# A state-space, Fourier and attention network on one core: ScalarE's deferred evictions, its long work and the last hy states

## The chip, the cores and the metric

The kernel runs on one core of one Trainium2 chip. The metric is the device time of one execution in microseconds, from the first instruction of the core to its last. All data is 32-bit floating point, apart from the two feed-forward blocks, which round to 8-bit and 16-bit formats as the reference does.

## The reference, cut to what matters

Four images of 64 x 64 tokens with 96 channels go through four layers.

- Layer 0: group norm, then a selective-scan block: an input projection, a 3 x 3 depthwise convolution with SiLU, scans in four directions, a layer norm, a gate and an output projection, plus the residual.
- Layer 1: a two-dimensional real Fourier transform (64 x 33 tokens, real and imaginary part as channels), the same kind of block, the inverse transform, plus the residual.
- Layers 2 and 3: linear attention and a quantized feed-forward block, with residuals.

The scans take nearly all of the time. In each direction, for each of 192 (layer 0) or 384 (layer 1) channels and each of 16 states:

```python
delta = softplus(dts + bias)
dA = exp(delta * A)
h = h * dA + (delta * u) * B        # a recurrence over the tokens
y = sum over the states of h * C
```

## The kernel before, in words

**Layout.** Channels lie on the 128 partitions in three groups (c = 0, 1, 2): in layer 0 two images share the partitions, in layer 1 one image fills them. Tokens lie along the free dimension. A direction is cut into segments: eight of 512 tokens in layer 0; 512, 512, 384, 384 and 320 in layer 1, in the opposite order for the two backward directions.

**Phases.** `scans` runs six phases: two pairs of images of layer 0, then four images of layer 1. Each has four directions. That makes 144 segments, and a segment has twelve steps: four state groups q of four states, times three channel groups c. There are 1728 steps in all: 1152 at 512 tokens, 384 at 384 and 192 at 320. Projection of the first pair stands ahead of the phases, and the tail of the last image (inverse transform, layers 2 and 3) behind them.

**One step** (the loop at the end of `scans`) has two pairs of states, hx and hy. VectorE runs the four scans (L546) and the product hcy = hy x C (L704). GpSimd computes hcx = hx x C (L686), copies the last hx and hy states of the segment for the next one (`keep_state`, L559), and fills the next step's hy with delta x u x B (`front_b`, L541). ScalarE computes the exponentials (L523) and scales bx (L498), which TensorE transposes into PSUM (L518). TensorE also transposes hcx and hcy and accumulates them over the states (L568). hx and hy have one buffer each. The banks for exponentials and transposes (`room`, tag "ab") are three, in rotation, so the exponential for the next step's first hy state waits for the last hy scan of this one.

**Order.** The engines' orders are fixed by the program (`manual_schedule`): each engine takes its instructions as the loop emits them. Other work is dealt out by generators in three slots of each step: `slot(None)` after the second hx scan, `slot(None)` between the two hy scans, and `slot(LATE)` ahead of hcy. A slot does two things:

- `prepare_more` takes one piece of `prepare`, which readies the next segment. Its pieces are: load u (three slots for the transfer), three matmuls of the x projection (L429), its eviction xs (L433), three products for delta (L439), each with an eviction (L442), the softplus over all three (L444, with a table load before and after), a transpose of xs (L450), its eviction bt (L455), du = delta x u on VectorE (L460), and three groups of transposes of du (L466) with evictions dut (L469). Products and transposes share one PSUM bank, tag "pp". At the start of the segment's last state group, whatever is left is drained at once.
- `E.step` takes one piece of the side task, such as projections and convolutions for later images (L146, L227), norm and gate (L310 to L354), the Fourier transforms (L833 to L896) or the attention and feed-forward blocks (`tokens`, L913 to L1063). It is taken when a counter, raised by a third of the phase's `RATES` entry in each slot, reaches one. Side work shares one PSUM bank, tag "ms". Its evictions are *deferred*: `E.defer` puts them on a list, and the next `E.step` issues them ahead of its own piece.

**Long work.** A softplus or SiLU needs another activation table. Such a piece is announced with `yield BURST` and runs only in `burst()`, which stands behind the step's exponentials and ahead of the second hx scan. In such a step (`long`), the bx work ahead of the hy scans is left out and follows later in the step.

Of the kernel before, what the change touches and what calls it, by code (L numbers as in the profile page):

```python
# [6 lines left out]
F32 = mybir.dt.float32  # L7
# [14 lines left out]
C, P = 3, 128  # L22
SM = 512
LATE, BURST = "late", "burst"

RATES = [0.71, 1.42, 2.55, 1.66, 1.66, 1.66]
EXP_LN = "natural_log_exp_and_others"


class Cfg:  # L30
# [5 lines left out]
    def __init__(self, pre, NI, KI, NR, nat, R, parts, rows, segs, eps):  # L36
        self.pre = pre
        self.NI, self.PI, self.KI = NI, P // NI, KI
        self.DI = C * self.PI
        self.NR, self.L, self.nat = NR, NR * 64, nat  # L40
        self.R, self.M = R, R + 2 * NST
        self.parts = parts
        self.rows = [(sum(rows[:i]), n) for i, n in enumerate(rows)]
        self.segs = [(sum(segs[:i]), n) for i, n in enumerate(segs)]
        self.eps = eps
# [11 lines left out]
class Env:  # L57
# [16 lines left out]
        self.finish()  # L74
        self.task, self.wants = task, None

    def step(self, kind):

        later, self.later = self.later, []
        for fn in later:  # L80
            fn()
        if self.task is None or self.wants not in (None, kind):
            return False
        try:
            self.wants = next(self.task)
        except StopIteration:
            assert not self.later
            self.task = None
        return True
# [277 lines left out]
class Seg:  # L367


    def __init__(self, ph, k, a, S, first, last):  # L370
        self.ph, self.blk, self.cfg = ph, ph.blk, ph.blk.cfg
        self.k, self.a, self.S, self.first, self.last = k, a, S, first, last
        self.rev = k >= 2
        self.nm = f"{self.cfg.pre}_{ph.g}_{k}_{a}"
        self.blocks = [(t, min(P, S - t)) for t in range(0, S, P)]
        full = S // P

        self.runs = [(0, full, P)] + ([(full, full + 1, S % P)] if S % P else [])
        self.bx, self.b, self.c = {}, {}, {}


class Step:
# [7 lines left out]
def scans(tc, ctx, phases, ident):  # L390
# [8 lines left out]
    nc = tc.nc  # L399
    NBK = SM // P  # L400
    NQ = NST // 4
    sp = ctx.enter_context(tc.tile_pool(name="scan", bufs=1))
    ps = ctx.enter_context(tc.tile_pool(name="scanps", bufs=1, space=PSUM))
    E = Env(tc, lambda name: ps.tile([P, 512], F32, name=name, tag="ms"))

    segs = []
    for ph in phases:
        for k in (0, 2, 1, 3):
            order = ph.blk.cfg.segs[::-1] if k >= 2 else ph.blk.cfg.segs
            segs += [Seg(ph, k, a, S, i == 0, i == len(order) - 1) for i, (a, S) in enumerate(order)]  # L410

    def prepare(z):


        blk, cfg, k, S, nm = z.blk, z.cfg, z.k, z.S, z.nm
        rows = cfg.NI * cfg.M

        def room():
            return ps.tile([P, 512], F32, name=f"pp_{nm}", tag="pp")

        z.u = u = sp.tile([P, C, SM], F32, name=f"us_{nm}", tag="us")
        nc.sync.dma_start(out=u[:, :, :S], in_=z.ph.io["u"][k % 2][:, :, z.a : z.a + S])
        z.xd = blk.dram_tile("xd", (rows, SM), nm, bufs=4)
        yield
        yield
        yield
        px = room()
        for c in range(C):
            nc.tensor.matmul(px[:rows, :S], blk.xpw[:, c, k, :], u[:, c, :S], start=(c == 0), stop=(c == C - 1))  # L429
            yield  # L430
        yield
        xs = sp.tile([P, SM], F32, name=f"xs_{nm}", tag="xs", bufs=2)
        nc.scalar.copy(xs[:rows, :S], px[:rows, :S])  # L433
        nc.sync.dma_start(out=z.xd[:, :S], in_=xs[:rows, :S])
        yield
        z.delta = sp.tile([P, C, SM], F32, name=f"delta_{nm}", tag="delta", bufs=2)
        for c in range(C):
            pd = room()
            nc.tensor.matmul(pd[:, :S], blk.dtw[:, k, c * P : (c + 1) * P], xs[:rows, :S], start=True, stop=True)  # L439
            yield  # L440
            yield
            nc.scalar.activation(z.delta[:, c, :S], pd[:, :S], AF.Identity, bias=blk.dtb[:, c, k : k + 1])  # L442
        yield BURST
        nc.scalar.activation(z.delta[:, :, :S], z.delta[:, :, :S], AF.Softplus)  # L444
        nc.scalar.preload_act_table_set(EXP_LN)
        yield
        pb = room()
        pbv = pb[:, : NBK * rows].rearrange("p (b m) -> p b m", b=NBK)
        for i, (t, n) in enumerate(z.blocks):
            nc.tensor.transpose(pbv[:n, i, :], xs[:rows, t : t + n], ident[:rows, :rows])  # L450
        z.bt = sp.tile([P, NBK, rows], F32, name=f"bt_{nm}", tag=f"bt{cfg.pre}", bufs=2)
        yield
        yield
        for lo, hi, n in z.runs:
            nc.scalar.copy(z.bt[:n, lo:hi, :], pbv[:n, lo:hi, :])  # L455
        yield
        yield
        yield LATE
        z.du = sp.tile([P, C, SM], F32, name=f"du_{nm}", tag="du", bufs=2)
        nc.vector.tensor_tensor(z.du[:, :, :S], z.delta[:, :, :S], u[:, :, :S], ALU.mult)  # L460
        yield
        z.dut = sp.tile([P, NBK, C, P], F32, name=f"dut_{nm}", tag="dut", bufs=2)
        for c in range(C):
            pt = room().rearrange("p (b d) -> p b d", b=NBK)
            for i, (t, n) in enumerate(z.blocks):
                nc.tensor.transpose(pt[:n, i, :], z.du[:, c, t : t + n], ident)  # L466
            yield
            for lo, hi, n in z.runs:
                nc.scalar.copy(z.dut[:n, lo:hi, c], pt[:n, lo:hi, :])  # L469
# [82 lines left out]
            ALU.add,  # L552
        )

    def keep_state(st, h, n0):
        z = st.z
        if not z.last:
            e = 0 if z.rev else z.S - 1
            nc.gpsimd.tensor_copy(  # L559
                z.state[st.c][:, n0 : n0 + 2].rearrange("p (j o) -> p j o", o=1), h[:, :, e : e + 1]  # L560
            )

# [43 lines left out]
    with tc.manual_schedule(engines=IN_ORDER):  # L606
# [3 lines left out]
        st = steps[0]  # L610
# [5 lines left out]
        bgen, pgen, pwants, at, due = make_bx(segs[0], 1), none, None, 0, 0.0  # L616

        def prepare_more(kind):

            nonlocal pwants  # L620
            if pwants not in (None, kind):
                return False
            pwants = next(pgen, LATE)
            return True

        def slot(kind):


            nonlocal due
            prepare_more(kind)  # L630
            due = min(due + st.z.ph.rate / 3, 3.0)
            if due >= 1.0:
                due -= E.step(kind)

        def burst():

            if pwants is BURST:
                return prepare_more(BURST)
            if E.wants is BURST:
                E.step(BURST)  # L640
                return True
            return False

        for i, st in enumerate(steps):
            z, q, c, S = st.z, st.q, st.c, st.z.S
            nxt = steps[i + 1] if i + 1 < len(steps) else None
            if q == 0 and c == 0:
                after = segs[at + 1] if at + 1 < len(segs) else None
                if at == 0 or z.ph is not segs[at - 1].ph:
                    if closing:  # L650
                        close_chunk(closing)
                        closing = None
                    z.ph.io["y"] = [z.blk.dram_tile(f"y{j}", (2, z.cfg.L, C * P), z.ph.g) for j in range(2)]
                    E.start(z.ph.side(E))
                open_segment(z, segs[at - 1] if at else None)
                if after and after.ph is not z.ph:
                    E.finish()
                pgen, pwants = prepare(after) if after else none, None
                at += 1
# [8 lines left out]
            hx = sp.tile([P, 2, SM], F32, name=f"hx_{st.nm}", tag="hx")  # L668
# [5 lines left out]
            long = burst()  # L674
# [9 lines left out]
                nxt.px = [transposed(nxt, 0)]  # L684
            hcx = sp.tile([P, 2, SM], F32, name=f"hcx_{st.nm}", tag="hcx", bufs=2)
            nc.gpsimd.tensor_tensor(hcx[:, :, :S], hx[:, :, :S], z.c[q][0][:, :, :S], ALU.mult)  # L686
            keep_state(st, hx, 4 * q)
            first = 0 if long else per - per // 2
            take(bgen, first)
            scan(st, st.hy, 0, st.ay[0], st.hy[:, 0], 4 * q + 2)  # L690
            if nxt:
                nxt.px.append(transposed(nxt, 1))
            slot(None)
            scan(st, st.hy, 1, st.ay[1], st.hy[:, 1], 4 * q + 3)
            keep_state(st, st.hy, 4 * q + 2)
            if nxt:
                front_y(nxt, 0)
            take(bgen, per - first)
# [369 lines left out]
def build(tc, ins, consts, out):  # L1068
    nc = tc.nc
    with ExitStack() as ctx:  # L1070
# [60 lines left out]
        with ExitStack() as inner:  # L1131
# [3 lines left out]
                [  # L1135
                    Phase(blk[0], 0, pairs[0], side((begin0, 1)), RATES[0]),
                    Phase(blk[0], 1, pairs[1], side((end0, 0), (begin1, 0), (begin1, 1)), RATES[1]),
                    Phase(blk[1], 0, single[0], side((end0, 1), (begin1, 2), (begin1, 3)), RATES[2]),
                    Phase(blk[1], 1, single[1], side((end1, 0)), RATES[3]),
                    Phase(blk[1], 2, single[2], side((end1, 1)), RATES[4]),  # L1140
                    Phase(blk[1], 3, single[3], side((end1, 2)), RATES[5]),
                ],
# [116 lines left out]
```

## Time and profile before

The median of three runs is 12,892.95 us (12,887.82 to 12,930.84).

| engine | busy, us | share of the span |
|---|---|---|
| TensorE | 9942.2 | 77% |
| VectorE | 10,425.9 | 81% |
| ScalarE | 9022.7 | 70% |
| GpSimd | 9126.6 | 71% |

| part of the span | us |
|---|---|
| ahead of the phases | 546 |
| phases 0 and 1 (layer 0) | 2559, 2639 |
| phases 2 to 5 (layer 1) | 1818, 1600, 1604, 1595 |
| behind the phases | 548 |

| group of instructions | count | busy, us | mean, ns |
|---|---|---|---|
| GpSimd hy product, L541 | 1728 | 3707.9 | 2146 |
| GpSimd hcx product, L686, its largest row | 1637 | 3558.6 | 2174 |
| GpSimd copy of hy states, L559 | 1392 | 1365.4 | 981 |
| GpSimd copy of hx states, L559 | 1392 | 322.2 | 231 |
| ScalarE table loads, L444 and L445 | 288 | 369.6 | 1283 |

PE is TensorE, DVE is VectorE, ACT is ScalarE, POOL is GpSimd, SP issues the transfers. A row of the profile's timeline gives start and duration in us, engine, line, operation, what is written and read, and in brackets the engine's idle time before it and what ended that. A row of the list of waits gives who waited for whom: us in total, number of times, the longest. L numbers are lines of the kernel before.

### The profile page before, as it was taken

The page shows a single profiled execution, that of the slowest core. Times are in us where ns is not written, and L with a number is a line of the kernel's source. Part 1 is how long each engine was busy: PE and PEld are TensorE (multiplying, and loading weights), DVE is VectorE, ACT ScalarE, POOL GpSimd, SP SyncE. Part 2 cuts the span into 40 slices and gives each one's busy share as a digit, 9 for nine tenths or more (in the row PEclk, how much of TensorE's full clock was granted, in tenths as well). Part 3 has the DMA queues.
Part 4 walks back from the last instruction along what each step waited for, and adds up shares of the span by engine and source line. Part 5 has one row for each costly group of instructions (what it writes and reads, how often), then busy time and mean ns, then how long its engine had stood idle before and what let it go on. Part 6 is the DMA issues. An engine that isn't in the chain of part 4 may idle for free.

```text
span 12908.9 us, 162342 instructions
## 1 busy us (share of the span) xinstructions
PE 9942.2 (77%) x54680; PEld 7205.1 (56%) x54680; DVE 10425.9 (81%) x10170; ACT 9022.7 (70%) x17333; POOL 9126.6 (71%) x6620
## 2 busy tenths in 40 slices
PE   4677777777777888878888878877788777887766
PEld 1355555555656666556655556555565555655544
DVE  1399999899999888898675688788987989879833
ACT  1478888888787888886565677677776777667723
POOL 0398989898888888886575687666876667766620
PEclk8788898888998999988798888777887778887775
DMA  4344444444555545544443344322433224432231
GB/s 119 104 128 121 123 119 124 116 117 130 144 138 129 135 126 129 140 133 140 124 129 102 120 135 116 101 79 80 135 114 97 80 83 134 113 100 78 81 96 26
DMA packets 1264685, 1464.23 MB, mean 113 GB/s; under 512 B 494243, under 2 KB 1027055, under 8 KB 1255143
## 3 DMA queue, kind: packets, MB, share of 16 engines
q1 hardware_dynamic: 1263847, 1453.85, 40.4%
q8 instruction: 430, 7.05, 0.2%
q14 instruction: 408, 3.34, 0.1%
HBM read 1217.05 MB, written 236.50 MB: 113 GB/s over the span
## 4 chain that ended last, share of the span: by engine, by line
PE 24%; DVE 23%; ACT 21%; POOL 20%; issue 7%; DMA 5%; SPq 0%; POOLq 0%; DVEq 0%; ACTq 0%
POOL hy_l L541 13%; DVE hy_l L546 12%; DVE hx_l L546 5%; PE pc_l L227 4%; ACT ax_l L523 4%; PE acc_l L568 4%; ACT bx_l L498 4%; POOL state_l L559 4%; DVE hcy_l L704 4%; POOL hcx_l L686 2%; ACT b_l L523 2%; PE b_l L518 2%; ACT ab_l L523 2%; PE pp_l L439 2%; PE pi_l L146 1%
## 5 line engine op out<-in xcount | busy, mean ns | idle before, releaser
L541 POOL TENSOR_TENSOR hy_l<-du_l,bc_l 128x1024 f32<-128x1024 f32 (+2 forms) x1728 | 3707.9, 2146 | 1526.5 <-DVE hcy_l L704 1056.2
L686 POOL TENSOR_TENSOR hcx_l<-hx_l,bc_l 128x1024 f32<-128x1024 f32 (+2 forms) x1637 | 3558.6, 2174 | 609.6 <-DVE hx_l L546 607.8
L498 ACT ACTIVATE bx_l<-dut_l,bt_l 128x192 f32<-128x192 f32 (+2 forms) x6272 | 2768.5, 497 | 0.0
L568 PE MATMUL acc_l<-ident,hcy_l 128*128 128x128 f32 (+1 forms) x12120 | 1888.6, 305 | 487.2 <-DVE hcy_l L704 483.9
L546 DVE TENSOR_TENSOR_SCAN hx_l<-ax_l,state_l,b_l 128x512 f32<-128x512 f32 (+2 forms) x1697 | 1839.1, 1125 | 390.2 <-PE b_l L518 315.9
L523 ACT ACTIVATE ax_l<-delta_l,l_alog 128x512 f32<-128x512 f32 (+2 forms) x3456 | 2138.6, 666 | 0.0
L523 ACT ACTIVATE b_l<-delta_l,l_alog 128x512 f32<-128x512 f32 (+2 forms) x1961 | 1229.9, 627 | 1282.9 <-DVE hx_l L546 886.0
L546 DVE TENSOR_TENSOR_SCAN hy_l<-b_l,state_l,hy_l 128x512 f32<-128x512 f32 (+2 forms) x1697 | 1858.3, 1130 | 257.5 <-POOL hy_l L541 126.9
L568 PEld LDWEIGHTS acc_l<-ident,hcy_l 128*128 128x128 f32 (+1 forms) x12120 | 1585.5, 157 | 854.5 <-DVE hcy_l L704 649.1
L568 PE MATMUL acc_l<-ident,hcx_l 128*128 128x128 f32 (+1 forms) x12126 | 1950.4, 311 | 123.8 <-POOL hcx_l L686 121.2
L568 PEld LDWEIGHTS acc_l<-ident,hcx_l 128*128 128x128 f32 (+1 forms) x12126 | 1619.7, 160 | 526.5 <-POOL hcx_l L686 253.1
L704 DVE TENSOR_TENSOR hcy_l<-hy_l,bc_l 128x1024 f32<-128x1024 f32 (+2 forms) x1636 | 1857.5, 1135 | 43.7
L559 POOL COPY state_l<-hy_l 128x2 f32<-128x2 f32 x1392 | 1365.4, 981 | 574.8 <-DVE hy_l L546 553.3
L518 PE MATMUL b_l<-ident,bx_l 128*128 128x128 f32 x6872 | 1240.2, 309 | 526.1 <-DVE hy_l L546 311.9
L523 ACT ACTIVATE ab_l<-delta_l,l_alog 128x512 f32<-128x512 f32 x1314 | 906.3, 690 | 998.6 <-DVE hx_l L546 707.3
L518 PEld LDWEIGHTS b_l<-ident,bx_l 128*128 128x128 f32 x6872 | 867.2, 155 | 1008.6 <-DVE hy_l L546 447.9
L546 DVE TENSOR_TENSOR_SCAN hy_l<-ab_l,state_l,hy_l 128x512 f32<-128x512 f32 x978 | 1205.8, 1269 | 130.7 <-POOL hy_l L541 75.1
L546 DVE TENSOR_TENSOR_SCAN hx_l<-ax_l,state_l,ab_l 128x512 f32<-128x512 f32 x979 | 1197.0, 1264 | 135.1 <-PE ab_l L518 102.1
L518 PE MATMUL ab_l<-ident,bx_l 128*128 128x128 f32 x5260 | 901.8, 307 | 520.9 <-DVE hy_l L546 266.5
L518 PEld LDWEIGHTS ab_l<-ident,bx_l 128*128 128x128 f32 x5260 | 653.1, 155 | 837.7 <-DVE hy_l L546 387.1
L227 PE MATMUL pc_l<-pad_l,l_dg 128*128 128x512 f32 (+2 forms) x1944 | 846.4, 578 | 58.2 <-ACT uh_l L216 42.8
L439 PE MATMUL pp_l<-xs_l,l_dtw 76*128 76x512 f32 (+3 forms) x864 | 525.2, 693 | 194.4 <-ACT delta_l L442 181.9
(190 smaller groups left out, 12231.5 us busy)
## 6 DMA issues: line engine op xcount, KB each, us to landing
bc_l<-l_xd_l SPq DMA_DIRECT2D x1536, 256.0 KB
bc_l<-l_xd_l SPq DMA_DIRECT2D x384, 512.0 KB
bc_l<-l_xd_l SPq DMA_DIRECT2D x384, 384.0 KB
us_l<-l_u SPq DMA_DIRECT2D x96, 768.0 KB
l_y<-y_l SPq DMA_DIRECT2D x288, 256.0 KB
bc_l<-l_xd_l SPq DMA_DIRECT2D x192, 320.0 KB
yt_l<-l_y SPq DMA_DIRECT2D x264, 192.0 KB
yt_l<-l_y SPq DMA_DIRECT2D x128, 384.0 KB
```

What stands on the lines that cost most here:

```text
L146: self.nc.tensor.matmul(out[i * cfg.PI : (i + 1) * cfg.PI, :n], wi[:, ki, half, :], xin[:, max(i, ki), :n], start=(ki == 0), stop=(ki == c ...
L227: nc.tensor.matmul(pc[:, : n * 64].rearrange("p (r w) -> p r w", w=64), diag[:, t, :], pad[:, r - p0 + dy : r - p0 + dy + n, dx : dx + 64] ...
L439: nc.tensor.matmul(pd[:, :S], blk.dtw[:, k, c * P : (c + 1) * P], xs[:rows, :S], start=True, stop=True)
L498: nc.scalar.activation(t[:n, b, :, ch], z.dut[:n, b, :, ch], AF.Copy, scale=z.bt[:n, b, m : m + 1])
L518: nc.tensor.transpose(pb[:, t : t + n], st.z.bx[st.q, j][:n, b, st.c], ident[:n, :n])
L523: nc.scalar.activation(out, z.delta[:, st.c, : z.S], AF.Exp, scale=z.blk.A[:, st.c, z.k, n : n + 1])
L541: nc.gpsimd.tensor_tensor(st.hy[:, :, :S], du, st.z.b[st.q][:, :, :S], ALU.mult)
L546: nc.vector.tensor_tensor_scan(h[:, j, : z.S][:, ::step], a[:, : z.S][:, ::step], b[:, : z.S][:, ::step], 0.0 if z.first else z.state[st.c ...
L559: nc.gpsimd.tensor_copy(z.state[st.c][:, n0 : n0 + 2].rearrange("p (j o) -> p j o", o=1), h[:, :, e : e + 1])
L568: nc.tensor.matmul(z.acc[st.c][:n, b, :], hc[:, j, t : t + n], ident, start=(n0 + j == 0 and b == 0), stop=(n0 + j == NST - 1 and b == 0), ...
L686: nc.gpsimd.tensor_tensor(hcx[:, :, :S], hx[:, :, :S], z.c[q][0][:, :, :S], ALU.mult)
L704: nc.vector.tensor_tensor(hcy[:, :, :S], st.hy[:, :, :S], z.c[q][1][:, :, :S], ALU.mult)
```

## The change

Five edits go together.

1. `flush` is split from `E.step`, and `burst()` calls it ahead of long work, so that deferred evictions stand in front of the softplus or SiLU on ScalarE and not behind it.
2. In a step with long work the middle slot only flushes; it takes no new piece and does not raise the counter. `RATES` is raised by about 3% to make up for it.
3. In `prepare` the delta products are taken apart: a slot lies between the eviction of one and the next product, which needs the same bank.
4. u of the next segment is loaded in the same phase as soon as du has been computed, the last reader of the one u buffer; its three slots of waiting then fall away.
5. The last hy states are copied by ScalarE; in a step with long work GpSimd still does it.

```diff
-RATES = [0.71, 1.42, 2.55, 1.66, 1.66, 1.66]
+RATES = [0.73, 1.47, 2.63, 1.72, 1.72, 1.72]
...
+    def flush(self):
         later, self.later = self.later, []
         for fn in later:
             fn()
+
+    def step(self, kind):
+        self.flush()
         if self.task is None or self.wants not in (None, kind):
             return False
...
+    def load_u(z):
+        z.u = sp.tile([P, C, SM], F32, name=f"us_{z.nm}", tag="us")
+        nc.sync.dma_start(out=z.u[:, :, : z.S], in_=z.ph.io["u"][z.k % 2][:, :, z.a : z.a + z.S])
...
-        z.u = u = sp.tile([P, C, SM], F32, name=f"us_{nm}", tag="us")
-        nc.sync.dma_start(out=u[:, :, :S], in_=z.ph.io["u"][k % 2][:, :, z.a : z.a + S])
         z.xd = blk.dram_tile("xd", (rows, SM), nm, bufs=4)
-        yield
-        yield
-        yield
+        if z.u is None:
+            load_u(z)
+            yield
+            yield
+            yield
+        u = z.u
...
             nc.scalar.activation(z.delta[:, c, :S], pd[:, :S], AF.Identity, bias=blk.dtb[:, c, k : k + 1])
+            if c < C - 1:
+                yield
         yield BURST
...
         nc.vector.tensor_tensor(z.du[:, :, :S], z.delta[:, :, :S], u[:, :, :S], ALU.mult)
+        if z.after and z.after.ph is z.ph:
+            load_u(z.after)
         yield
...
-        def slot(kind):
+        def slot(kind, hold=False):
             nonlocal due
+            if hold:
+                E.flush()
+                return
             prepare_more(kind)
...
         def burst():
+            if BURST in (pwants, E.wants):
+                E.flush()
             if pwants is BURST:
                 return prepare_more(BURST)
...
-            keep_state(st, hx, 4 * q)
+            keep_state(nc.gpsimd.tensor_copy, st, hx, 4 * q)
...
-            slot(None)
+            slot(None, hold=long)
             scan(st, st.hy, 1, st.ay[1], st.hy[:, 1], 4 * q + 3)
-            keep_state(st, st.hy, 4 * q + 2)
+            keep_state(nc.gpsimd.tensor_copy if long else nc.scalar.copy, st, st.hy, 4 * q + 2)
```

More of the change, by code (lines that the diff above doesn't have):

```diff
@@ L75, in start @@
         self.task, self.wants = task, None
-    def step(self, kind):
+    def flush(self):
         later, self.later = self.later, []
@@ L378, in __init__ @@
         self.runs = [(0, full, P)] + ([(full, full + 1, S % P)] if S % P else [])
-        self.bx, self.b, self.c = {}, {}, {}
+        self.bx, self.b, self.c, self.u, self.after = {}, {}, {}, None, None
 class Step:
@@ L410, in scans @@
             segs += [Seg(ph, k, a, S, i == 0, i == len(order) - 1) for i, (a, S) in enumerate(order)]
+    for z, after in zip(segs, segs[1:]):
+        z.after = after
+    def load_u(z):
+        z.u = sp.tile([P, C, SM], F32, name=f"us_{z.nm}", tag="us")
+        nc.sync.dma_start(out=z.u[:, :, : z.S], in_=z.ph.io["u"][z.k % 2][:, :, z.a : z.a + z.S])
     def prepare(z):
@@ L553, in scan, with keep_state @@
         )
-    def keep_state(st, h, n0):
+    def keep_state(copy, st, h, n0):
         z = st.z
@@ L558, in keep_state @@
             e = 0 if z.rev else z.S - 1
-            nc.gpsimd.tensor_copy(
+            copy(
                 z.state[st.c][:, n0 : n0 + 2].rearrange("p (j o) -> p j o", o=1), h[:, :, e : e + 1]
@@ L647, in scans @@
             if q == 0 and c == 0:
-                after = segs[at + 1] if at + 1 < len(segs) else None
+                after = z.after
                 if at == 0 or z.ph is not segs[at - 1].ph:
```

## The prediction

> **What bounds the kernel now.** I read the page's totals first.
>
> ```profile
> span 12908.9 us, 162342 instructions
> PE 9942.2 (77%) x54680; PEld 7205.1 (56%) x54680; DVE 10425.9 (81%) x10170; ACT 9022.7 (70%) x17333; POOL 9126.6 (71%) x6620
> PE 24%; DVE 23%; ACT 21%; POOL 20%; issue 7%; DMA 5%; SPq 0%; POOLq 0%; DVEq 0%; ACTq 0%
> ```
>
> No engine is full, and the chain that ended last is shared by four. So the bound is a ring of waits. The timeline of one quiet 512-token step shows it; GpSimd first, then VectorE over the same stretch.
>
> ```profile
> 3008.56 0.19 POOL L559 COPY state_l<-hx_l 128x2 f32<-128x2 f32 x1
> 3008.92 1.17 POOL L559 COPY state_l<-hy_l 128x2 f32<-128x2 f32 x1 [0.17 <-DVE hy_l L546]
> 3010.19 2.37 POOL L541 TENSOR_TENSOR hy_l<-du_l,bc_l 128x1024 f32<-128x1024 f32 x1
> ```
>
> ```profile
> 3006.33 2.46 DVE L546 TENSOR_TENSOR_SCAN hy_l<-ab_l,state_l,hy_l 128x512 f32<-128x512 f32 x2 [0.16 <-POOL hy_l L541]
> 3008.82 1.23 DVE L704 TENSOR_TENSOR hcy_l<-hy_l,bc_l 128x1024 f32<-128x1024 f32 x1
> 3012.59 1.28 DVE L546 TENSOR_TENSOR_SCAN hy_l<-ab_l,state_l,hy_l 128x512 f32<-128x512 f32 x1 [0.18 <-POOL hy_l L541]
> ```
>
> hy has one buffer: hcy (1.23) must end before GpSimd refills hy (2.37), then come two scans (2.46), then the next hcy. With the gaps that is 6.26 us, from one hy scan to the next. The same sum gives about 4.9 us at 384 tokens and 4.2 at 320. Quiet steps everywhere would take 1152 x 6.26 + 384 x 4.9 + 192 x 4.2 = 9900 us; the six phases take 11,815 (windows 546 to 12,361). So 1915 us are disturbance, and only there can the edits gain. Outside the phases nothing is edited.
>
> The worst kind is a step with ScalarE's long work in it ("long step"). At 8789 us, ScalarE, then TensorE, then VectorE:
>
> ```profile
> 8789.40 1.28 ACT L444 ACT_TABLE_LOAD   x1
> 8790.69 1.16 ACT L444 ACTIVATE delta_l<-delta_l 128x1152 f32<-128x1152 f32 x1
> 8791.87 1.28 ACT L445 ACT_TABLE_LOAD   x1
> 8793.17 0.58 ACT L1016 COPY xt<-pt 97x512 f32<-97x512 f32 x1
> 8797.19 0.53 ACT L523 ACTIVATE b_l<-delta_l,l_alog 128x320 f32<-128x320 f32 x1 [3.43 <-DVE hy_l L546]
> ```
>
> ```profile
> 8793.81 2.02 PE L1020 MATMUL pao<-wo,xt 97*128 97x96 f32 x8 [4.08 <-ACT xt L1016]
> ```
>
> ```profile
> 8795.86 0.55 DVE L1022 TENSOR_TENSOR tok<-tok,pao 128x384 f32<-128x384 f32 x1 [6.20 <-PE pao L1020]
> ```
>
> The deferred eviction L1016 sits behind 3.7 us of long work, the next product waits for it, and the addition, placed between the two hy scans, stops VectorE for 6.20 us. The list of waits gives the whole run's size:
>
> ```profile
> DVE hx_l L546 <- PE b_l L518: 353.3, 146, 11.5
> PE pp_l L439 <- ACT delta_l L442: 181.9, 158, 4.8
> DVE tok L1022 <- PE pao L1020: 78.6, 33, 6.2
> ```
>
> **What the Trainium skill says.** "GPSIMD Engine Reference", Specifications: GpSimd shares its SBUF interfaces with VectorE and contends with VectorE instructions that have two SBUF inputs. The trace agrees: the same 128x2 copy takes 0.19 us after hcx and 1.17 us beside hcy, a two-input operation, and ends 0.04 us after it. "TensorE: Matmul & The Clock Gate", Architectural detail: ScalarE and VectorE take their queues strictly first in, first out. The trace agrees (L1016 above). "ScalarE: Activation LUTs", What ACT_TABLE_LOAD costs: a load is about 1283 ns; the trace shows 1.28 us.
>
> **The change part by part.**
>
> *Evictions ahead of the long work, middle slot empty.* The trace has 178 long steps in the phases: 143 with a softplus, 35 with a SiLU. Of their cost, the long work itself and the product du (L460, 1.74 us at 512 tokens, ahead of hcy) stay. What can go is waiting for an eviction stuck behind it. I went through the trace step by step. In the last three phases VectorE's side operations wait in long steps for L1022 33.5 us (6 times), L937 28.1 (9), L1059 18.2 (6), L1041 9.5 (3): 89 us, 30 a phase. In the changed program's order I looked for side operations of VectorE that depend on ScalarE work placed after the long work: per phase L1022 and L1059 fall from two each to none, L937 from three to two, L1041 goes from one to two, and one L896 appears. At about 3.1 us each that is 16 us a phase; gain 3 x 14 = 42. One step later, hx scans stand behind a TensorE queue stopped at a stuck eviction: L799 15.5, L836 11.4, L216 11.7, L200 7.5, of which half of the last remains: gain 42. L775 in phases 1 and 2: about 12. Against it, two more projections (L433) come to lie behind a SiLU: 4 lost. Gain **92 us**. The extra flush itself costs nothing: the same copy, earlier.
>
> *Delta products apart, next u loaded early.* The product no longer follows its own bank's eviction within a slot, so the 182 us row falls to near nothing. TensorE has slack, so little of it is on the path: hx scans of the step before the long work wait 116 us for transposes in all, of which 24 are named L439 or L442, and some more are side products in the same slot. I take **35 us**; ends 5 (named evictions alone) and 80. The load of u moves to just after du, its last reader; it waits at most for that product on the DMA queue, and the broadcasts behind it are due steps later: nothing. The three saved slots less two new ones leave the long work at step 5 of the segment; the empty slot moves du one step on, and the last copy of dut into the drain at step 9, where ScalarE otherwise waits for hx: nothing. But each phase's first segment has no early load; it gets 16 slots ahead of the softplus, and all three transposes of dut fall into the drain, a chain of about 3 x (0.5 + 0.6) us on TensorE and ScalarE, five times: **16 us lost**.
>
> *Last hy states copied by ScalarE.* 1290 copies leave GpSimd. Busy, that is over 1000 us; on the path it is nothing, since hcy ends when the copy ends and the refill needs hcy too. A segment that keeps no state proves it:
>
> ```profile
> 3028.96 2.36 POOL L541 TENSOR_TENSOR hy_l<-du_l,bc_l 128x1024 f32<-128x1024 f32 x1 [1.57 <-DVE hcy_l L704]
> ```
>
> hcy there runs 3027.59 to 3028.82: refill 0.14 us later, as with the copy (3010.05 to 3010.19). On ScalarE the copy costs about 0.2 us (nearest row: L960, 128x8, 208 ns; the skill's price, same section, 186 + 0.833 x 2 = 188 ns). The exponential behind it waits for the same scan already. But the refill now waits for ScalarE: exp, two exps, bx, slot evictions are queued ahead. In a 512-token step ScalarE arrives 0.8 us before the scan ends, with 1.2 us of hcy more to hide in. Taking, step by step, ScalarE's measured arrival plus 0.25 us in place of GpSimd's copy, the refill delays the hy scan in 64 of the 1291 steps, by 46 us in all. Ends: 20 (later evictions absorb it) and 150 (0.25 us in each of some 560 steps where ScalarE is late at this point). I take **50 us lost**.
>
> *Rates.* Held slots do not count, and the side work ends at the same step of each phase in the changed order, so no tail is added. Outside long steps side steps lie a little closer (0.573 a slot for 0.553), so neighbouring ones meet more often: **8 us lost**.
>
> Sum: -92 - 35 + 16 + 50 + 8 = -53 us, **12,840 us**.
>
> **The rivals.** *Larger gain*: disturbances feed each other (a late bx delays the next transposes), and removing one frees more than its own wait. For it: long steps and the three after them hold some 1100 us over the quiet pace. Against: most of that is du, TensorE busy with convolutions (L227), and ScalarE's own 4 us. Gain 92 + 80, times 1.2, less 50: about 12,735. *Cancelled*: new alignments make new waits of the same kind; the last three phases run one pattern, so each counts three times. 12,885. *Slower, the wait moved*: the state copy puts ScalarE into the ring in its busy steps. For it: 560 late steps, and short steps have under 1 us to hide it. Against: the measured arrivals. Loss 150 + 16 + 30, gains of 130: 12,960.
>
> **How the numbers follow.** Forecast 0.50, larger gain 0.13, cancelled 0.20, slower 0.17. The range 12,730 to 12,950 takes in the larger gain's centre and the slower case's near half; a fifth is left out. 0.3% is 39 us: below 12,854 lie the larger gain and most of the forecast, 0.56; within, 0.24; above 12,932, 0.20.
>
> **What would show it.** Right: GpSimd near 8000 us busy; no 6 us wait at L1022; the L439 row on L442 near zero; quiet steps still 6.26 us; refills waiting for hcy, not for ScalarE. Wrong: a row of refills waiting for the state copy on ScalarE above 100 us, quiet steps of another length, or side operations waiting as long in long steps as before.

## The result, and the profile after

The kernel after takes **12,836.47 us** (median of four runs, 12,824.57 to 12,858.33) where the kernel before takes 12,898.67 (median of four, 12,887.82 to 12,930.84). The ratio is 0.995 with a 95% interval of 0.9927 to 0.9972, so about 62 us are gained. A later run of the same kernel on another chip gave 0.9953 (0.9941 to 0.9966).

Line numbers move in the kernel after: hy refill L541 becomes L557, scans L546 are L562, hcy L704 is L725, state copies L559 are L575, transposes L518 are L534, delta products and evictions L439 and L442 are L451 and L454, softplus L444 is L458, transposes and evictions of dut L466 and L469 are L482 and L485, and the side operations L1016, L1020, L1022 are L1037, L1041, L1043.

The page's totals, and three of its costliest groups (busy us, mean ns, then idle time before them and what ended it):

```profile
span 12839.4 us, 162267 instructions
PE 9948.5 (77%) x54680; PEld 7174.4 (56%) x54680; DVE 10477.0 (82%) x10170; ACT 9133.9 (71%) x18623; POOL 7885.6 (61%) x5330
L557 POOL TENSOR_TENSOR hy_l<-du_l,bc_l 128x1024 f32<-128x1024 f32 (+2 forms) x1728 | 3709.4, 2147 | 3549.2 <-DVE hcy_l L725 1944.7
L725 DVE TENSOR_TENSOR hcy_l<-hy_l,bc_l 128x1024 f32<-128x1024 f32 (+2 forms) x1636 | 1890.9, 1156 | 43.8
L575 ACT COPY state_l<-hy_l 128x2 f32<-128x2 f32 x1246 | 236.6, 190 | 573.9 <-DVE hy_l L562 507.8
```

GpSimd lost 1241 us of busy time (9126.6 to 7885.6) and ScalarE gained 111. The time fell by 62, and e2 below shows that emptying GpSimd alone gave nothing. The ring still sets the quiet step: two hcy starts, and the refill between them.

```profile
3005.66 1.22 DVE L725 TENSOR_TENSOR hcy_l<-hy_l,bc_l 128x1024 f32<-128x1024 f32 x1
3011.91 1.22 DVE L725 TENSOR_TENSOR hcy_l<-hy_l,bc_l 128x1024 f32<-128x1024 f32 x1
```

```profile
3007.03 2.36 POOL L557 TENSOR_TENSOR hy_l<-du_l,bc_l 128x1024 f32<-128x1024 f32 x1 [1.58 <-DVE hcy_l L725]
```

That is 6.25 us a step, as before. What changed is the long step. At 8766 us the deferred eviction L1037 stands ahead of the table loads and not behind them; ScalarE, TensorE, VectorE:

```profile
8765.93 0.56 ACT L1037 COPY xt<-pt 97x512 f32<-97x512 f32 x1
8766.52 1.28 ACT L458 ACT_TABLE_LOAD   x1
8767.81 1.16 ACT L458 ACTIVATE delta_l<-delta_l 128x1152 f32<-128x1152 f32 x1
8768.99 1.28 ACT L459 ACT_TABLE_LOAD   x1
```

```profile
8766.55 1.13 PE L1041 MATMUL pao<-wo,xt 97*128 97x96 f32 x8 [1.06 <-ACT xt L1037]
```

```profile
8767.72 0.55 DVE L1043 TENSOR_TENSOR tok<-tok,pao 128x384 f32<-128x384 f32 x1 [1.38 <-PE pao L1041]
```

The addition waits 1.38 us where the same one waited 6.20. Summed step by step over the last three phases, VectorE's side operations in long steps wait 28 us for 89 before. The list of waits shows that other waits grew at the same time:

```profile
POOL hy_l L557 <- ACT state_l L575: 584.5, 203, 11.7
ACT dut_l L485 <- PE pp_l L482: 288.2, 221, 8.2
DVE hx_l L562 <- PE b_l L534: 253.5, 132, 11.1
DVE tok L1043 <- PE pao L1041: 49.0, 39, 3.3
PE pp_l L451 <- ACT delta_l L454: 31.4, 15, 4.2
```

Down are the hx scans' waits for transposes (353.3 to 253.5), the additions to tok (78.6 to 49.0) and the delta products' waits for evictions (181.9 to 31.4). Up, from 119.6 us, is the second row: evictions of dut on ScalarE that wait for their transposes. The first row is new. The hy scans' wait for refills has hardly moved (294.6 us before):

```profile
DVE hy_l L562 <- POOL hy_l L557: 287.4, 1276, 2.9
```

### The profile page after: what moved, and what is told of

Same layout as the page of the kernel before. It is cut to its first block, busy times and chain, and to the rows that moved or that the text cites. A ratio compares the mean times of both kernels' runs of the same rounds, so it can differ in the third digit from the quotient of the medians.

```text
span 12839.4 us, 162267 instructions
## 1 busy us (share of the span) xinstructions
PE 9948.5 (77%) x54680; PEld 7174.4 (56%) x54680; DVE 10477.0 (82%) x10170; ACT 9133.9 (71%) x18623; POOL 7885.6 (61%) x5330
## 5 line engine op out<-in xcount | busy, mean ns | idle before, releaser
L557 POOL TENSOR_TENSOR hy_l<-du_l,bc_l 128x1024 f32<-128x1024 f32 (+2 forms) x1728 | 3709.4, 2147 | 3549.2 <-DVE hcy_l L725 1944.7
L562 DVE TENSOR_TENSOR_SCAN hx_l<-ax_l,state_l,b_l 128x512 f32<-128x512 f32 (+2 forms) x1696 | 1838.2, 1125 | 307.5 <-PE b_l L534 240.0
L562 DVE TENSOR_TENSOR_SCAN hy_l<-b_l,state_l,hy_l 128x512 f32<-128x512 f32 (+2 forms) x1697 | 1861.6, 1131 | 276.1 <-ACT b_l L539 143.0
L725 DVE TENSOR_TENSOR hcy_l<-hy_l,bc_l 128x1024 f32<-128x1024 f32 (+2 forms) x1636 | 1890.9, 1156 | 43.8
L534 PE MATMUL b_l<-ident,bx_l 128*128 128x128 f32 (+1 forms) x6868 | 1249.2, 309 | 569.6 <-DVE hy_l L562 320.7
L534 PEld LDWEIGHTS b_l<-ident,bx_l 128*128 128x128 f32 (+1 forms) x6868 | 866.5, 155 | 1033.4 <-DVE hy_l L562 463.1
L534 PE MATMUL ab_l<-ident,bx_l 128*128 128x128 f32 x5264 | 911.5, 308 | 589.0 <-DVE hy_l L562 300.1
L562 DVE TENSOR_TENSOR_SCAN hy_l<-ab_l,state_l,hy_l 128x512 f32<-128x512 f32 x978 | 1208.2, 1270 | 166.8 <-ACT ab_l L539 87.1
L562 DVE TENSOR_TENSOR_SCAN hx_l<-ax_l,state_l,ab_l 128x512 f32<-128x512 f32 x980 | 1198.2, 1264 | 91.5 <-PE ab_l L534 58.8
L534 PEld LDWEIGHTS ab_l<-ident,bx_l 128*128 128x128 f32 x5264 | 648.2, 154 | 892.2 <-DVE hy_l L562 413.8
L575 ACT COPY state_l<-hy_l 128x2 f32<-128x2 f32 x1246 | 236.6, 190 | 573.9 <-DVE hy_l L562 507.8
L474 DVE TENSOR_TENSOR du_l<-delta_l,us_l 128x1536 f32<-128x1536 f32 (+2 forms) x144 | 231.8, 1610 | 426.1 <-ACT delta_l L458 426.1
```

Of the source, the lines that this page charges most:

```text
L534: nc.tensor.transpose(pb[:, t : t + n], st.z.bx[st.q, j][:n, b, st.c], ident[:n, :n])
L557: nc.gpsimd.tensor_tensor(st.hy[:, :, :S], du, st.z.b[st.q][:, :, :S], ALU.mult)
L562: nc.vector.tensor_tensor_scan(h[:, j, : z.S][:, ::step], a[:, : z.S][:, ::step], b[:, : z.S][:, ::step], 0.0 if z.first else z.state[st.c ...
L575: copy(z.state[st.c][:, n0 : n0 + 2].rearrange("p (j o) -> p j o", o=1), h[:, :, e : e + 1])
L725: nc.vector.tensor_tensor(hcy[:, :, :S], st.hy[:, :, :S], z.c[q][1][:, :, :S], ALU.mult)
```

## The experiments

The theory to be tested is the prediction's sum: the flush and the held slot gain 92, products apart 35, the ScalarE copies cost 50. The main rivals are that the copies cost nothing and another edit gives the gain back, and that gains and losses sit in other edits than the sum has them. Every ratio is to the kernel before, run on the same chip. 0.1% is 13 us.

**e1: after, with GpSimd copying all states.**

```diff
-            keep_state(nc.gpsimd.tensor_copy if long else nc.scalar.copy, st, st.hy, 4 * q + 2)
+            keep_state(nc.gpsimd.tensor_copy, st, st.hy, 4 * q + 2)
```

> The kernel after with one part undone: GpSimd copies the last hy states in every step, as before. Theory 1 (the prediction's: the copy on GpSimd was free behind hcy, on ScalarE it costs refills): 50 to 110 us faster than the kernel after, that is 112 to 170 us under the kernel before, 12,730 to 12,790; refills 0.14 us after hcy nearly everywhere. Rival 2 (the copy's removal helps GpSimd as much as it harms, since the copies of ut between it and the refill no longer wait for it): within 25 us of the kernel after, about 12,836. Rival 3 (it is the gain): slower than the kernel after.

Measured: 12,808.18 us, 0.993 (0.9916 to 0.9944). By the two runs of the kernel after, the copies on ScalarE cost it some 0.2%, 26 to 30 us, less than theory 1's 50 to 110. Those runs are of other chips and the intervals overlap, so that even this cost is likely and not certain.

**e2: before, with the same copies on ScalarE.** The edit is the last line of the diff alone.

> The kernel before with one part done alone: ScalarE copies the last hy states except in long steps. Theory 1: 30 to 100 us slower than the kernel before, 12,930 to 13,000, and about 1100 us less busy time on GpSimd all the same. Rival 2: within 25 us of it. Rival 3: 30 to 100 us faster.

Measured: 12,895.2 us, 0.9996 (0.9988 to 1.0004). Alone the edit costs nothing, although its list of waits has a large row:

```profile
POOL hy_l L541 <- ACT state_l L559: 418.7, 126, 14.1
ACT dut_l L469 <- PE pp_l L466: 108.0, 79, 4.9
```

Counted from the traces, what refills start later than 0.15 us after the end of hcy grows from 73 us before, of which 63 stand behind copies of ut (GpSimd's side work), to 230 in e2, 165 of it in phase 2. But the hy scans, which need the refill, do not wait for it longer. First the row of the kernel before, then that of e2:

```profile
DVE hy_l L546 <- POOL hy_l L541: 294.6, 1206, 2.5
```

```profile
DVE hy_l L546 <- POOL hy_l L541: 260.4, 1217, 2.5
```

So in the steps in which the refill is late, VectorE is mostly held by something else as well. The waits behind copies of ut fall from 63 us to 15, since the state copy no longer stands in GpSimd's queue: the copy of ut now starts with hcy or just ahead of it, and the refill is free when hcy ends. But hcy pays. In the kernel after (VectorE, then GpSimd):

```profile
1172.93 1.70 DVE L725 TENSOR_TENSOR hcy_l<-hy_l,bc_l 128x1024 f32<-128x1024 f32 x1
```

```profile
1172.93 0.62 POOL L250 COPY ut_l<-uh_l 128x256 f32<-128x256 f32 x1
1174.78 2.36 POOL L557 TENSOR_TENSOR hy_l<-du_l,bc_l 128x1024 f32<-128x1024 f32 x1 [1.23 <-DVE hcy_l L725]
```

hcy takes 1.70 us here where 1.22 is usual; over the 93 cases at 512 tokens in which such a copy has begun before hcy and still runs when it starts, its mean is 1.58. All hcy average 1157 ns in e2 and 1156 in the kernel after, 1135 in e1: 21 ns in 1636 is 34 us. So the edit takes one delay away and makes hcy slower, and in e2 the time is the same.

**e3: before, with the flush, the held slot and the new rates.**

```diff
+            if BURST in (pwants, E.wants):
+                E.flush()
...
-            slot(None)
+            slot(None, hold=long)
```

> The kernel before with the flush ahead of long work, the held middle slot and the new rates alone. Theory 1: 80 to 110 us faster than before, about 12,800; no 6 us wait of VectorE at the token addition in long steps. Rival 2 (waits only move to other steps): 20 to 50 us faster. The whole change gained 62 us, so with states and prepare at plus 34 in sum, this part would be near minus 95.

Measured: 12,905.4 us, 1.0004 (0.9996 to 1.0012). The predicted gain of 92 is not there, and neither is the rival's 20 to 50.

**e4: before, with products apart and the early load of u.** Edits 3 and 4 of the change.

> The kernel before with the delta products apart and u loaded early alone. Theory 1: -35 for the products and +16 for the first segments of phases, so about 20 us faster, 12,880; the wait of the delta products for their evictions near zero. Rival 2: the products are off the path, within 10 us of before or 15 us slower. Rival 3: they are the larger half of the gain, 60 us faster.

Measured: 12,865.92 us, 0.9971 (0.996 to 0.9983), a gain of 37 by the ratio and 29 by the medians, for 20 expected.

**e5: before, with the flush alone.** e3 without the held slot, at the old rates.

> The kernel before with the flush ahead of long work alone: the middle slot is not held, the rates are the old ones. In e3 (flush, held slot and new rates) the last three phases came out some 40 us shorter, phases 1 and 2 some 55 us longer. Theory H (the held slot and the new rates cost, the flush gains): e5 is 40 to 60 us faster than before, phases 1 and 2 within 10 us of before. Theory P (the loss in phases 1 and 2 comes from the flush itself, or from the products that still follow their own evictions): within 15 us of before, phase 2 again 20 us or more longer.

Measured: 12,839.13 us, 0.9956 (0.9944 to 0.9968), a gain of 57. The flush gains, and what came with it in e3, the held slot and the new rates, gave back 0.48%, 62 us. The lists of waits show where. First e3, then e5 (its last row is read further below):

```profile
ACT dut_l L480 <- PE pp_l L477: 313.5, 237, 10.4
DVE hy_l L557 <- ACT b_l L534: 215.0, 170, 6.1
```

```profile
ACT dut_l L473 <- PE pp_l L470: 132.0, 106, 4.9
DVE hy_l L550 <- ACT b_l L527: 149.7, 145, 6.0
DVE hx_l L550 <- PE b_l L522: 326.7, 151, 11.3
```

The three evictions of dut of a segment can be placed by ScalarE's own order, by the exponentials around each (steps 0 to 11; the drain stands at the start of step 9, the first of the last state group). Before, the first stands in the middle slot of step 7, the second in the last slot of step 7, the third in the first slot of step 8. du may run only in the last slot of a step. So one slot lost between the softplus and du costs du a whole step, and all three evictions move on by one step: the third falls into the drain, straight behind the second. The kernel after shows it (ScalarE, then TensorE):

```profile
2742.73 0.69 ACT L539 ACTIVATE b_l<-delta_l,l_alog 128x512 f32<-128x512 f32 x1
2743.35 0.58 ACT L485 COPY dut_l<-pp_l 128x512 f32<-128x512 f32 x1
2744.68 0.59 ACT L485 COPY dut_l<-pp_l 128x512 f32<-128x512 f32 x1 [0.75 <-PE pp_l L482]
2745.16 0.70 ACT L539 ACTIVATE b_l<-delta_l,l_alog 128x512 f32<-128x512 f32 x1
```

```profile
2743.98 0.66 PE L482 MATMUL pp_l<-ident,du_l 128*128 128x128 f32 x4 [0.47 <-ACT dut_l L485]
```

The third group of transposes needs the bank that the second eviction reads, and the third eviction needs the transposes; ScalarE stands still meanwhile, with the next exponential of hy behind it.

| kernel | softplus, mostly in step | the three evictions, in step | ScalarE waits for transposes before the third, us in all | ratio to before |
|---|---|---|---|---|
| before | 5 | 7, 7, 8 | 3.9 | 1 |
| e5, flush alone | 5 | 7, 7, 8 | 5.4 | 0.9956 |
| e4, products apart and early u | 5 | 7, 7, 8 | 10.0 | 0.9971 |
| e6 (below): e4 and e5 | 5 | 7, 7, 8 | 8.3 | 0.9919 |
| e3, flush and held slot | 5 | 8, 8, drain | 156.0 | 1.0004 |
| e1, after with GpSimd states | 5 | 8, 8, drain | 159.9 | 0.993 |
| after | 5 | 8, 8, drain | 156.5 | 0.995 |
| e7, products apart alone | 6 | 8, 8, drain | 157.7 | 1.0013 |
| e9, early u alone | 4 | 6, 6, 7 | 9.8 | 0.9963 |
| e10, flush and early u | 4 | 6, 6, 7 | 9.1 | 0.9864 |

The steps hold for most segments; in the kernels with the early u, the first segment of a phase has no early load, and its steps come later. In e3 the exponentials of hy, queued behind the drain on ScalarE, keep VectorE waiting 215.0 us where e5 has 149.7. That the drain makes up all of the 62 us is argued and not shown, since the rates were changed too and a held slot also moves side work.

**e6: after, without the held slot, at the old rates, with GpSimd copying all states.** That is before with the flush, products apart and the early u.

> The kernel after without the held slot, with the old rates, and with GpSimd copying the states: the prepare edits plus the flush. Theory H: 15 to 40 us faster than e1 (0.993 of before), about 0.990, phases 1 and 2 about 15 us shorter each than in e1. Theory P: within 15 us of e1, or slower where evictions made in the middle slot behind the long work stop TensorE (about 0.995).

Measured: 12,795.52 us, 0.9919 (0.9906 to 0.9933). The gains of e4 and e5 nearly add up (0.29% and 0.44%; together 0.81%). Against e1 the held slot and the rates cost 0.11% here, less than theory H's 15 to 40 us, but on two chips and within their intervals.

**e7: before, with products apart alone.**

```diff
+            if c < C - 1:
+                yield
```

> The kernel before with a slot between each delta eviction and the next product, and nothing else; u is still loaded at the start of its segment, so the softplus comes two slots later. e4 (this and the early load of u) gained 29 us by medians. If the products are the gain: 25 to 40 us faster than before, and the wait of L439 for L442 near zero. If the early load (a shorter preparation) is needed as well: within 15 us of before, since du and its transposes then fall into the drain at the last state group.

Measured: 12,911.03 us, 1.0013 (1.0006 to 1.0019), a loss of 17. Its list of waits:

```profile
ACT dut_l L471 <- PE pp_l L468: 271.7, 240, 7.0
PE pp_l L439 <- ACT delta_l L442: 19.8, 11, 3.9
```

The wait that the edit is aimed at falls from 181.9 us to 19.8, and the run is slower. But the two slots more also move the softplus a step on and the third eviction of dut into the drain. The run mixes a wait taken away with a drain made, and so it does not show what the wait was worth.

**e8: after, with two buffers for hy.** To make room, two tiles of layers 2 and 3 (lnq and xt in `tokens`) have one buffer in place of two.

```diff
-        st.hy = sp.tile([P, 2, SM], F32, name=f"hy_{st.nm}", tag="hy")
+        st.hy = sp.tile([P, 2, SM], F32, name=f"hy_{st.nm}", tag="hy", bufs=2)
```

> The kernel after with two buffers for hy, which takes away the wait of the refill for hcy and for the state copy; to make room, layers 2 and 3 have one buffer each for the squares and the transposed tokens where they had two. If hy's ring of hcy, refill and two scans sets the quiet step, the step falls from 6.26 us to VectorE's own five operations, about 6.1 us, at 512 tokens, and refills no longer wait for ScalarE's copy: 60 to 200 us faster than the kernel after. If VectorE or GpSimd alone set it, the step stays 6.26 us and the kernel is within 30 us of the kernel after.

Measured: 13,264.21 us, 1.0285 (1.0271 to 1.03), about 430 us more than the kernel after (0.995, on another chip), where the expectation had a gain or nothing. The timeline of the same quiet step, and the row of hcy on the page:

```profile
3009.33 1.23 DVE L725 TENSOR_TENSOR hcy_l<-hy_l,bc_l 128x1024 f32<-128x1024 f32 x1
3015.47 1.23 DVE L725 TENSOR_TENSOR hcy_l<-hy_l,bc_l 128x1024 f32<-128x1024 f32 x1
```

```profile
L725 DVE TENSOR_TENSOR hcy_l<-hy_l,bc_l 128x1024 f32<-128x1024 f32 (+2 forms) x1636 | 2227.9, 1362 | 43.8
```

The ring was real: the quiet step is 6.14 us, and the quickest tenth of 512-token steps falls from 6.24 to 5.97. But the one buffer had also kept hcy and the refill apart. With two, they run into each other. Where the refill starts ahead (202 cases at 512 tokens), hcy takes 2.58 us on average, up to 3.47, in place of 1.22; where the refill starts inside hcy (209 cases), it takes 3.36 us itself, in place of 2.36. The mean of all hcy rises from 1156 to 1362 ns (337 us of VectorE), and that of the refill from 2147 to 2327 (311 us of GpSimd). The smaller buffers of layers 2 and 3 may bear on the result too, and the granted clock of TensorE in the profiled run was 0.829, where it was 0.848 in the kernel after; neither share was measured.

**e9: before, with the early load of u alone.** e4 without the slot between products.

> The kernel before with u loaded early alone; products still follow their own evictions, so the softplus comes three slots earlier than before. e7 (products apart alone) was 17 us slower, e4 (both) 37 us faster. Theory Q (the products' waits are off the path; the gain is the earlier softplus and du): 30 to 60 us faster, 12,835 to 12,865, with the 182 us wait of products for evictions unchanged. Theory R (the products gain about 40 us, and e7 lost it again because two more slots push the transposes of dut into the drain): within 15 us of before. ScalarE's wait for the transposes of dut should be about 120 us, as in all kernels whose dut ends ahead of the drain.

Measured: 12,855.84 us, 0.9963 (0.995 to 0.9975), a gain of 48.

```profile
PE pp_l L451 <- ACT delta_l L454: 193.4, 166, 6.8
ACT dut_l L483 <- PE pp_l L480: 53.1, 44, 4.8
```

The products' waits are all still there, and the gain is as large as e4's. The three slots that the load no longer holds let softplus, du and dut run a step earlier than before, and ScalarE's waits for the transposes of dut fall from 119.6 us to 53.1, where 120 was expected.

This can't be what e4 gained by, since there softplus and dut stand in the same steps as before. Three pairs in the table differ by edits 3 and 4 alone and have the same steps: before and e4, e5 and e6, e3 and e1. The two edits together gain 37, 48 and 95 us in them. So it is not shown that the products' waits were worth nothing; as much as the prediction's 35 us is possible. The rival is that the x projection and the transfers come earlier. No run has the products apart at unchanged steps and u loaded late, and this stays open.

**e10: before, with the flush and the early u.** e6 without the slot between products.

> e6 (products apart, early u, flush, GpSimd states; 0.9919 of before) without the products apart. Theory Q: as fast as e6 within 15 us, 0.991 to 0.993. Theory R: 30 to 50 us slower than e6, about 0.995, as the flush alone.

Measured: **12,728.55 us, 0.9864** (0.985 to 0.9878). It beats both kernels, the one before by 1.36% or 175 us (167 by the medians), and it is faster than either theory had it.

```profile
PE pp_l L451 <- ACT delta_l L454: 192.9, 160, 6.9
DVE hy_l L560 <- ACT b_l L537: 94.8, 98, 5.5
ACT dut_l L483 <- PE pp_l L480: 66.4, 52, 7.9
```

The fastest kernel of the study keeps the whole of the wait that edit 3 takes away. Beside it, e6, with the products apart, takes 0.55% longer, some 70 us. The table gives what goes with it (in e10 the softplus is at step 4 and dut at 6 and 7, a step earlier than in e6), and the hy scans' wait for exponentials is 94.8 us in e10 and 139.4 in e6. That this earlier place is the whole cause is argued, not shown: no kernel moved du alone. The two gains are also worth more together (1.36%) than apart (0.44% and 0.37%).

**e11: after, with the middle slot in use and the old rates.**

```diff
-            slot(None, hold=long)
+            slot(None)
```

> The kernel after with the middle slot in use in long steps and the old rates; ScalarE copies the states. Theory D (the held slot costs by pushing the transposes of dut into the drain; states on ScalarE cost 26 us only together with it): 10 to 30 us faster than the kernel after, 12,805 to 12,825, ScalarE's wait for dut back to about 130 us from 288. If states on ScalarE cost by themselves: 25 us slower than e6 (12,796). If they cost nothing there: equal to e6 within 10 us.

Measured: 12,780.49 us, 0.991 (0.9894 to 0.9925).

```profile
POOL hy_l L557 <- ACT state_l L575: 446.2, 149, 15.1
ACT dut_l L485 <- PE pp_l L482: 128.9, 87, 4.9
```

**e12: after, unchanged, on the chip of e11.**

> The kernel after itself, on the same chip as the three others, as their measure: 0.993 to 0.997 of before by its first runs.

Measured: 12,837.6 us, 0.9953 (0.9941 to 0.9966). So the held slot and the rates cost the kernel after 0.43%, some 55 us, where theory D had 10 to 30, and the wait of dut's evictions falls from 283.6 us to 128.9 without them. With the middle slot in use, the ScalarE copies cost nothing (e11 at 0.991 beside e6 at 0.9919). That they cost only where the drain holds ScalarE up as well would fit e1, but the loss there is too small to show it.

## Why the prediction was right, and which of its steps were not

The time came within 4 us of the forecast, and the sum was -62 for -53. That closeness is luck: the mechanism of the flush holds, but most sizes do not, and their errors cancelled. Taken in this order, e5, e6, e11 and e12 give each part (the first two ran on one chip, the last two on another):

| part | predicted, us | measured, us |
|---|---|---|
| flush | -92, with the held slot | -57 (e5) |
| products apart, early u | -35 + 16 = -19 | -48 (e5 to e6) |
| state copies on ScalarE | +50 | -12, not clear of noise (e6 to e11) |
| held slot and new rates | +8, for the rates | +55 (e11 to e12) |
| sum | -53 | -62 |

- **Flush.** The mechanism is right: the 6.20 us wait is gone. With the flush alone, side waits in long steps of the last three phases fall from 89 us to 43, close to the 42 counted. The step that failed is the size of the other half: the row of hx scans' waits for transposes falls by 27 us (353.3 to 326.7), where 42 were counted.
- **"The last copy of dut into the drain at step 9 ... nothing."** This is the step that failed worst. The place was right, the price was not: I took ScalarE to be free there. The third eviction waits for its transposes some 156 us in all instead of 4, ahead of exponentials that VectorE needs. The held slot and the rates cost 62 us (e3 less e5) and 55 (e12 less e11). These runs don't separate the two, but e7 has old rates and no held slot, and shows the same drain.
- **Products apart, -35.** Alone +17, and beside e10, where u is early and the flush is there, +70; but both times later pieces move on by a step. At equal steps, products apart and the early u together gain 37 to 95. The prediction saw that the added slots are paid for by the saved ones. It gave no price to the slots themselves, and e10, which keeps the saved ones, is 70 us faster than e6.
- **Early load of u, nothing for itself and +16 for the first segments.** Without the two added slots it gains 48 (e9), or some 119 on top of the flush (e5 to e10). The loss in the first segments was not measured by itself.
- **ScalarE copies, +50.** 0 alone (e2), and some 28 in the kernel after, if anything. Late refills were expected to delay hy scans; refills start late by 213 us in all in the kernel after and by 73 before, but hy scans wait for refills no longer (294.6 us before, 287.4 after). What was missed lies on GpSimd: copies of ut no longer hold up the refill (39 us in phases 0 and 1 before, 6 after), and slow hcy instead.
- **The rivals.** "Larger gain" had the right idea, that disturbances feed each other, for another kernel: e10's two edits give 175 where apart they give 105. "Cancelled" describes what the held slot does to the flush in e3. "Slower" rested on ScalarE's copies, and no run supports its 150 us.

Of the signs set out beforehand, four came true: GpSimd at 7885.6 us, no 6 us wait at the addition, the products' row down to 31.4, quiet steps at 6.25. One came out as the sign of being wrong: refills wait for ScalarE 584.5 us, far above 100. The sign was badly chosen, since a row of waits counts from the engine's last work, and does not tell whether anyone needed the engine by then. A late refill in the kernel after shows it (VectorE, ScalarE, GpSimd):

```profile
8773.68 0.82 DVE L725 TENSOR_TENSOR hcy_l<-hy_l,bc_l 128x640 f32<-128x640 f32 x1
8777.48 0.55 DVE L1043 TENSOR_TENSOR tok<-tok,pao 128x384 f32<-128x384 f32 x1 [1.54 <-PE pao L1041]
8777.95 1.53 DVE L562 TENSOR_TENSOR_SCAN hy_l<-b_l,hy_l 128x320 f32<-128x320 f32 x2
```

```profile
8774.81 0.56 ACT L1037 COPY xt<-pt 97x512 f32<-97x512 f32 x1
8775.27 0.19 ACT L575 COPY state_l<-hy_l 128x2 f32<-128x2 f32 x1
```

```profile
8775.54 1.54 POOL L557 TENSOR_TENSOR hy_l<-du_l,bc_l 128x640 f32<-128x640 f32 x1 [2.37 <-ACT state_l L575]
```

hcy ends at 8774.50, but the copy stands behind an eviction, and the refill comes at 8775.54. Of the 2.37 us in brackets, only the last 1.04 are after hcy. And even these cost nothing here: the refill ends at 8777.08, while the addition ahead of the hy scans holds VectorE until 8777.95.

## What to carry to other kernels

When an edit adds or removes places in a hand-dealt order, price where each later piece lands, above all against a point where the rest is drained at once; here a held slot, with rates 3% higher, decided between a gain of 57 us and none. A wait row is a cost only as far as it reaches past everything else that the next engine waits for: a new row of 418.7 us cost nothing in e2, and that of 584.5 some 30 us at most. But a row that went away in a slower run (181.9 us, e7) isn't shown to be worthless either, if the edit moved other pieces as well. Try each edit of a bundle alone and in pairs: two of the five made a kernel 0.9% faster than all five.

## What the runs showed of the hardware that I had not expected

VectorE and GpSimd slow each other in either direction, and in these runs the one that starts later pays. The prediction used only one side: a 128x2 copy of GpSimd that starts during hcy takes 1.17 us. The Trainium skill, "GPSIMD Engine Reference", Specifications, names the contention, and the runs agree and give sizes for the other side: hcy takes 1.58 us on average beside a 128x256 or 128x264 copy of GpSimd that started shortly before it, and 2.58 with a 128x1024 product of GpSimd started ahead of it (e8), for 1.22 undisturbed. The product takes 3.36 us, for 2.36, where it is the one that starts inside hcy. So a short GpSimd copy that starts behind hcy did hcy no harm (1.22 us in the kernel before), and taking it away made hcy slower by 34 us in all, since another copy came to start with it.
